# A filter bank turned earlier, PSUM banks in three pools, and a last stage that moves its final sums from SBUF to SBUF

## The chip, the core and the metric

The kernel runs on one core of a Trainium2 chip. The metric is device time in microseconds of one launch. One execution was also recorded by the hardware profiler; its "span" runs from the first to the last instruction. In what follows PE is TensorE, DVE is VectorE, ACT is ScalarE, POOL is GpSimd, and SP is the engine that issues nearly all DMAs; each takes its instructions in order. Tensors named `ud`, `xa`, `md`, `me` and `yd` lie in DRAM; all else that is named is in SBUF or, with a prefix `ps` or `p`, in PSUM. All numbers are float32.

## The reference, cut to what matters

The input is 8 sequences of 1024 tokens with 128 channels. Three blocks follow each other, each with a residual: a cosine-similarity attention of 4 heads, two state-space scans (forward and backward), and a spectral filter layer. The change touches the last one, and the last one only:

```python
Vf = jnp.fft.rfft(phi, n=n, axis=0)                 # 16 filters
Uf_p = jnp.fft.rfft(u, n=n, axis=1)                 # tokens, normalised
U_plus = jnp.fft.irfft(Vf[None, :, :, None] * Uf_p[:, :, None, :], n=n, axis=1)[:, :sl]
...
out = jnp.einsum('btkd,k,kde->bte', U_plus, s, Mpp) # and the same with (-1)^t
out = out + sum_i einsum('btd,de->bte', shift(u, i), Mu[i])   # 3 taps
x = t + out
```

So each of 16 filters convolves every channel causally over the whole sequence, a 128 x 128 matrix per filter mixes the channels, and the filters' results are added up.

## The kernel before, in words

The kernel exchanges the order: it mixes the filters first. For each of 128 frequencies it builds a 128 x 128 matrix (real and imaginary part, for both halves of the sequence), multiplies the spectra of the tokens by it, and transforms the product back. A sequence is cut into 2 blocks (`NB`, index `k`) of 512 tokens, and these into 4 interleaved parts (`r` or `q`) of 128. The tail of `fast_kernel` does this in two parts, and inside both the programs of all five engines are in the order in which the code is written (`manual_schedule(engines=ALL_IN_ORDER)`), so a place in the code is a place in each engine's queue.

**Spectra (pools `f_...`, from L1611).** A loop runs over the sequences b = 2 to 8. `transform(b)` (L1641) turns the normalised tokens on PE (`cpt`), and for each block multiplies them by the Fourier table `fwd` (`pf`); ACT and DVE take the results out, POOL adds them to the spectrum `sp`, and `store_spectra` writes it to `ud`. `copy_turned` (L567, two ACT copies) brings the turned tokens to `ut`, for the 3 taps (`taps_of`, L602, `pu`), whose sums DVE adds to the residual `X` (L612), and `store_residual` (L615) writes that to `xa`. In PSUM, `ps_f` has two buffers of two banks, `ps_o` two of one bank, `ps_t` one of two banks.

Between these, the 16 filters' matrices are prepared in four banks: `turned(n)` (L1624) transposes bank n on PE (`mdt`), DVE copies it (`me`), SP stores it to `me` in DRAM, and `spread(n)` (L1634) loads it back into its place in `mst` with four DMAs (L1636). `turned` runs at b = 3 to 6 between the two halves of the taps; `spread` at b = 4 to 7, first thing in the pass. So on SP the order of a pass is: `mst` of one bank, `ud`, `me` of the next bank, `xa`. In the pass b = 8 the first two of the eight steps of chunk 0's frequency matrices are made (L1595, PE; `gs` copies by ACT L1608 and DVE L1606), and these need all of `mst`.

**The loop over chunks (pools `g_...`, from L1708).** The 128 frequencies are in 16 chunks of 8. In a pass the matrices of the next chunk are made (`matrices`), 4 PSUM banks at a time, and between them come four products of this chunk (`apply`, L1727, `py`; n = 0 to 3, two to each half of the chunk's 8 frequencies). `gather` turns `py` into `sums`; `store` writes those of a half to `yd` (L1755), `fetch` (L1765) brings a part of them back with frequencies in partitions: only for piece 0, to `early_yt`. `amid_products` puts stores, fetches and the loads of the next spectra `u` (L1578) at a place on SP, by a wait for the middle of a product. A chunk holds every 16th frequency: its rows of `yd` and of `early_yt` lie 16 apart. All 8 PSUM banks are one pool, `g_ps_g`, which is opened when the three pools of the part before close.

**The last stage.** Four pieces (k, h), each of one block of four sequences: z = sums and differences of the piece's parts (DVE, L1831), 16 products by the inverse table `inv` (L1841, `pz`), DVE adds them to the residual (L1848), ACT issues the output's DMA (L1851). Pieces 1 to 3 are loaded from `yd` with two 1 MB DMAs each (L1825) into a room named `gs`; the residuals come from `xa` (L1782): 3 MB at the start of the last chunk, 1 MB behind piece 2.

Of the kernel before, what the change touches and what calls it, by code (L numbers as in the profile page):

```python
# [45 lines left out]
def fast_kernel(ctx: ExitStack, tc: tile.TileContext, a: dict, out: bass.AP, bad: bass.AP):  # L46
# [273 lines left out]
    def transforms(pool, tables):  # L320


        def over_2048(t):
            nc.vector.tensor_scalar(t, t, 1.0 / 2048.0, None, ALU.mult)

        odd = counted(pool, [2, NF // FC, FC], [[512, 2], [2, NF // FC], [2 * NF // FC, FC]], 1, 0, "odd")
        odd = odd.rearrange("p i c f -> p i (c f)")
        place = counted(pool, [4], [[1, 4]], 0, 4, "place")
        over_2048(place)
        by_place = [(fwd[:, k : k + 1], odd[:, 0:1, :], place[:, k : k + 1]) for k in range(4)]  # L330
        turns(by_place[:2])
        yield
        odd_row = counted(pool, [1], [[1, 1]], 1, 2, "odd_row")
        places = counted(pool, [4, P], [[1, 4], [4, P]], 0, 0, "places")
        over_2048(odd_row)
        yield
        turns(by_place[2:])
        yield
        for _ in angles(pool, fwd, "fwd"):
            yield  # L340
        yield
        turns([(inv, places, odd_row[:, 0:1])])
        for _ in angles(pool, inv, "inv"):
            yield
        yield
        lag = counted(pool, [2, 2], [[-256, 2], [1, 2]], 510, -2, "lag")
        over_2048(lag)
        for h in range(2):
            for r in range(2):
                t = pool.tile([P, 2, 2, NF], F32, name=f"lags{h}_{r}")  # L350
                turns([(t, odd, lag[:, h, r : r + 1])])
                for _ in angles(pool, t, f"lags{h}_{r}"):
                    pass
                tables.append(t)
                yield
        for t in tables:
            sines(t)

    def transform_taps(pool, ps, tables):
# [31 lines left out]
        nc.vector.tensor_reduce(sgn, late, AX.X, ALU.add)  # L391
        nc.vector.tensor_scalar(sgn, sgn, 1.0, None, ALU.add)
        nc.vector.tensor_tensor(weight[:, 1:2], weight[:, 0:1], sgn, ALU.mult)
        alt = pool.tile([P, NF // FC // 2, 2, FC], F32, name="alt")
        nc.gpsimd.memset(alt, 1.0)
        nc.gpsimd.memset(alt[:, :, 1], -1.0)
        alt = alt.rearrange("p c i f -> p (c i f)")

        both = pool.tile([P, NB, 512], F32, tag="work_w", name="taps_s")
        for m in range(NB):  # L400
# [191 lines left out]
    def store_spectra(b, sp):  # L592
        nc.sync.dma_start(
            ud[:, :, b].rearrange("c p k i q f -> p c (k i q f)"), sp.rearrange("p c k i q f -> p c (k i q f)")
        )
# [16 lines left out]
        nc.vector.scalar_tensor_tensor(xq[:, k], po, keep[:, k : k + 1], xq[:, k], ALU.mult, ALU.add)  # L612

    def store_residual(b):
        nc.sync.dma_start(xa[b].rearrange("p k r c -> p (k r) c"), X[b])  # L615

# [934 lines left out]
    with ExitStack() as s:  # L1553
# [10 lines left out]
            return u  # L1564

        def behind(instruction, other):
            tc.add_manual_dep(
                instruction.ins,
                other.ins.name,
                mybir.DependencyInfo(mybir.DependencyClass.Sync, mybir.DependencyReason.DATA),  # L1570
                reason="a place in the quarter",
            )

        def load_part(u, c, part, other=None):

            k, h = divmod(part, 2)
            bs = slice(4 * h, 4 * h + 4)
            t = nc.sync.dma_start(  # L1578
                u[:, 0, k, bs].rearrange("p b i f -> p b (i f)"), ud[c][:, bs, k].rearrange("p b i q f -> p b (i q f)")
            )  # L1580
            if other:
                behind(t, other)
            nc.gpsimd.tensor_scalar(u[:, 1, k, bs, 0, :], u[:, 0, k, bs, 1, :], -1.0, None, ALU.mult)  # L1583
            nc.gpsimd.tensor_copy(u[:, 1, k, bs, 1, :], u[:, 0, k, bs, 0, :])

# [25 lines left out]
        with ExitStack() as s2:  # L1611
# [8 lines left out]
                mds[n] = pm.tile([P, 8, C], F32, tag="md", name=f"md{n}")  # L1620
                nc.sync.dma_start(mds[n], md.rearrange("d r k e -> d (r k) e")[:, n::4, :])

            def turned(n):

                if n == 0:
                    load_bank(3)
                pt = ps_t.tile([P, 8, C], F32, tag="t", name=f"mdt{n}")
                for i in range(8):
                    nc.tensor.transpose(pt[:, i, :], mds[n][:, i, :], ident)
                to = p2.tile([P, 8, C], F32, tag="me", name=f"me{n}")  # L1630
                nc.vector.tensor_copy(to.rearrange("p k d -> p (k d)"), pt.rearrange("p k d -> p (k d)"))
                nc.sync.dma_start(me[:, n], to)

            def spread(n):  # L1634
                for g in range(4):
# [5 lines left out]
            def transform(b):  # L1641
# [7 lines left out]
                for k in range(NB):  # L1649
                    pf = ps_f.tile([P, 4, 2, NF], F32, tag="f", name=f"pf{b}_{k}")  # L1650
                    sd = p2.tile([P, 2, 2, 2, NF], F32, tag="sd", name=f"sd{b}_{k}")
                    later = p2.tile([P, 2, 2, NF], F32, tag="later", name=f"later{b}_{k}")
                    for _ in block_spectra(k, un, pf, sd, later, sp):
                        pass
                store_spectra(b, sp)
                copy_turned(uts[b], pt)

            def taps_of(b, k):
                po = ps_o.tile([P, 4, C], F32, tag="o", name=f"pu{b}_{k}")
# [23 lines left out]
            for b in range(2, B + 1):  # L1683
# [10 lines left out]
                if b > 2:  # L1694
                    taps_of(b - 1, 0)
                ahead(b, 1)
                if 3 <= b <= 6:
                    turned(b - 3)
                if b > 2:
                    taps_of(b - 1, 1)  # L1700
# [8 lines left out]
        with ExitStack() as s2:  # L1709
# [1 line left out]
            p3 = s2.enter_context(tc.tile_pool(name="g_3", bufs=3))  # L1711
            second_gs = s2.enter_context(tc.tile_pool(name="g_g", bufs=1))
            yp = s2.enter_context(tc.tile_pool(name="g_y", bufs=1, side="right"))
            early_yt = yp.tile([P, 2, 4, 4, C], F32, name="early_yt")
            ps_g = s2.enter_context(tc.tile_pool(name="g_ps_g", bufs=8, space=PSUM))

            def single_banks(c, n):
                return [ps_g.tile([P, 4, P], F32, tag="g", name=f"pg{c}_{n}_{g}") for g in range(4)]

            def apply(c, n, q, gs, u, py):  # L1720

# [27 lines left out]
                nc.vector.tensor_tensor(sums[:, 1, :], both[:, 0, :], both[:, 1, :], ALU.subtract)  # L1749
                stored[c, n] = sums  # L1750

            def store(c, n, other=None):

                at = c + n * 4 * chunks
                t = nc.sync.dma_start(  # L1755
                    yd[at :: chunks][:4].rearrange("f k b i q e -> f (k b i) (q e)"),
                    stored.pop((c, n)).rearrange("p q e -> p (q e)"),
                )
                if other:
                    behind(t, other)  # L1760

            def fetch(c, i, other=None):

                rows = slice(c, NF, chunks)
                t = nc.sync.dma_start(early_yt[rows, i], yd[rows, 0, 0:4, i])  # L1765
                if other:
                    behind(t, other)

            def amid_products(c, n, made):

                if n == 0 and c > 0:
                    store(c - 1, 1, made)
                if n == (3 if c + 1 < chunks else 2):
                    store(c, 0, made)
                if c + 1 < chunks and n in (1, 2):
                    for part in (2 * n - 2, 2 * n - 1):
                        load_part(us[c + 1], c + 1, part, made)
                if c > 0 and n > 1:
                    fetch(c - 1, n - 2, made)

            def load_residuals(k, b, n):
                nc.sync.dma_start(  # L1782
                    res[k][:, b : b + n].rearrange("p b r c -> p b (r c)"),
                    xa[b : b + n, :, k].rearrange("b p r c -> p b (r c)"),
                )

            chunks = NF // FC
            gathered, stored = {}, {}
# [1 line left out]
            for c in range(-1, chunks):  # L1790
# [4 lines left out]
                else:  # L1795
# [1 line left out]
                    room = chunk_matrices(c + 1, first_gs)  # L1797
                    res = [room[:, :32, :], mp.tile([P, 32, C], F32, tag="mst", name="res1")]
                    res = [t.rearrange("p (b r) c -> p b r c", b=B) for t in res]
                    load_residuals(1, 0, B)  # L1800
                    load_residuals(0, 0, 4)

                for n in range(4):
                    if c + 1 < chunks:
# [2 lines left out]
                                matrices(c + 1, i, gs[c + 1], single_banks(c + 1, i))  # L1807
                    if c >= 0:
                        half, turn = divmod(n, 2)
                        py = ps_g.tile([P, 2, C], F32, tag="g", name=f"py{c}_{n}")  # L1810
                        amid_products(c, n, apply(c, half, turn, gs[c], us[c], py))
                        apply(c, half, turn + 2, gs[c], us[c], py)
                        gather(c, half, turn, py)
            store(chunks - 1, 1)
            for i in range(2):
                fetch(chunks - 1, i)


            pieces = [(k, h) for k in range(NB) for h in range(2)]
            yts = [early_yt]  # L1820
            for n, (k, h) in enumerate(pieces[1:], 1):

                yts.append(room[:, 32 * n : 32 * n + 32].rearrange("p (i b q) c -> p i b q c", i=2, b=4))
                for i in range(2):
                    nc.sync.dma_start(yts[n][:, i], yd[:, k, h * 4 : h * 4 + 4, i])  # L1825
                if n == 2:
                    load_residuals(0, 4, 4)
            for yt, (k, h) in zip(yts, pieces):
                z = (second_gs if h else first_gs).tile([P, 2, 2, 4, C], F32, tag="u", name=f"z{k}_{h}")
                for r, i, op in ((0, 0, ALU.subtract), (0, 1, ALU.add), (1, 0, ALU.add), (1, 1, ALU.subtract)):  # L1830
                    nc.vector.tensor_tensor(z[:, r, i], yt[:, i, :, 2, :], yt[:, 1 - i, :, 3, :], op)  # L1831
# [3 lines left out]
                for b in range(0, 4, size):  # L1835
                    bs = slice(b, b + size)
                    to = res[blk][:, h * 4 + b : h * 4 + b + size]
                    for r in (0, 2, 1, 3):
                        po = ps_g.tile([P, 4, C], F32, tag="g", name=f"pz{k}_{h}_{b}_{r}")[:, :size]
                        for i in range(2):  # L1840
                            nc.tensor.matmul(  # L1841
                                po,
# [820 lines left out]
```

## Time and profile before

| | us |
|---|---|
| median of 3 runs (range) | 1401.44 (1399.33 to 1406.55) |
| the profiled execution | 1398.1 |
| its span | 1396.4 |
| PE busy in the span | 1324.2 (95%) |
| PE busy, 1140 to 1300, in the loop over chunks | 159.77 of 160 |
| PE busy, 1060 to 1100, entry to the loop | 34.95 of 40 |
| PE busy, 1300 to 1340 / 1340 to 1360 | 38.21 of 40 / 2.36 of 20 |
| PE busy, 1360 to 1380 / 1380 to the end | 20.00 of 20 / 9.23 of 16.4 |

A line of the timeline gives the start and length in us, the engine, the line of the kernel, what is written and read (partitions x elements), how many instructions were merged, and in brackets the idle time ahead of it with what ended it. SPq and ACTq lines are issues of DMAs by SP and ACT: their length is that of the issuing, not of the transfer. `[... <-issue]` means that the engine waited for nothing that the profile shows. In the view of stretches, each row has the busy time (and count) of PE, PE's weight loads, DVE, ACT and POOL, and then PE's granted clock (1 is full speed), the mean busy share of the 16 DMA engines, and GB/s.

### The profile page before, as it was taken

How to read it: one execution, taken by the hardware profiler on the slowest of the kernel's cores; microseconds unless marked ns; L12 is line 12 of the kernel's file. 1: busy time of each engine (PE TensorE's matmuls, PEld its weight loads, DVE VectorE, ACT ScalarE, POOL GpSimd, SP SyncE). 2: the span in 40 equal slices, each digit the busy share in tenths (PEclk: the TensorE clock that was granted, in tenths of full speed). 3: DMA queues.
4: the chain of work that ended last, by engine and by line, in shares of the span. 5: the costliest groups of instructions: out<-in, count | busy, mean ns of one | idle time of the engine just before them, and what ended most of it. 6: DMA issues, size and time to landing. Idle time of an engine off the chain costs nothing. (4 is left out here: it accounts for less than half of the span.)

```text
span 1396.4 us, 47738 instructions
## 1 busy us (share of the span) xinstructions
PE 1324.2 (95%) x20926; PEld 839.8 (60%) x20926; DVE 1102.8 (79%) x2144; ACT 922.4 (66%) x1428; POOL 552.4 (40%) x606
## 2 busy tenths in 40 slices
PE   7999999999999899999999999998998999999947
PEld 3333333333333566666666666666897999999934
DVE  5789889788868688889898888899764777777725
ACT  4766666766757788888888888886452555555510
POOL 3411986876910343434343433442883111111100
PEclk8999999999999999999999999999999999999979
DMA  7100111111000533444444543442476232333258
GB/s 182 47 2 2 35 43 39 54 39 39 24 9 12 126 77 78 108 93 103 96 107 95 120 92 92 93 92 61 141 246 203 52 74 75 76 75 81 73 173 301
DMA packets 143168, 123.25 MB, mean 88 GB/s; under 512 B 45000, under 2 KB 122440, under 8 KB 138856
## 3 DMA queue, kind: packets, MB, share of 16 engines
q1 hardware_dynamic: 140824, 115.93, 32.2%
q8 instruction: 166, 2.72, 0.8%
q10 hardware_dynamic: 2128, 4.19, 0.8%
q14 instruction: 50, 0.41, 0.1%
HBM read 78.15 MB, written 34.08 MB: 80 GB/s over the span
## 5 line engine op out<-in xcount | busy, mean ns | idle before, releaser
L810 ACT ACTIVATE pr<-pt 128x1024 f32<-128x1024 f32 x256 | 248.2, 1021 | 106.5 <-PE pt L805 105.5
L1608 ACT COPY gs<-pg 128x512 f32<-128x512 f32 x256 | 132.5, 602 | 67.7 <-PE pg L1595 67.0
L835 DVE TENSOR_TENSOR two<-pr,pr 128x1024 f32<-128x1024 f32 x128 | 164.9, 1329 | 15.5 <-ACT pr L810 15.5
L1606 DVE COPY gs<-pg 128x512 f32<-128x512 f32 x256 | 158.8, 685 | 18.9 <-PE pg L1595 10.8
L805 PE MATMUL pt<-q,k 32*128 32x512 f32 x1024 | 163.7, 656 | 6.1 <-ACT pr L810 4.2
L1595 PE MATMUL pg<-taps,mst 32*128 32x128 f32 x4096 | 148.1, 280 | 5.5 <-DMA mst<-me 2.9
L1595 PEld LDWEIGHTS pg<-taps,mst 32*128 32x128 f32 x4096 | 134.5, 187 | 19.2 <-issue 12.1
L826 PE MATMUL po<-pr,v 128*32 128x512 f32 x1024 | 141.1, 612 | 0.0
L1727 PE MATMUL py<-gs,u 128*32 128x128 f32 (+1 forms) x4096 | 128.4, 277 | 2.7 <-issue 2.7
L1031 POOL TENSOR_TENSOR ec<-ec,ct 128x2048 f32<-128x2048 f32 x16 | 83.6, 5227 | 112.4 <-ACT ct L1111 49.8
L1073 DVE SCALAR_TENSOR_TENSOR xs<-xp,cw,xs 128x1024 f32<-128x1024 f32 x96 | 122.5, 1282 | 2.2 <-issue 0.2
L1583 POOL TENSOR_SCALAR u<-u 128x128 f32<-128x128 f32 x64 | 34.2, 534 | 223.7 <-DMA u<-ud 188.6
L1727 PEld LDWEIGHTS py<-gs,u 128*32 128x32 f32 (+1 forms) x4096 | 112.1, 140 | 10.5 <-issue 2.9
L1095 PE MATMUL pb<-bxt,wbc 128*128 128x512 f32 x256 | 114.0, 597 | 3.6 <-ACT zs L1086 3.6
L805 PEld LDWEIGHTS pt<-q,k 32*128 32x128 f32 x1024 | 50.2, 188 | 89.7 <-ACT pr L810 27.2
L1303 POOL TENSOR_TENSOR rms<-rms_v,mhalf 128x8 f32<-128x8 f32 x16 | 26.6, 1660 | 157.0 <-DVE rms_v L1301 157.0
L1194 DVE SCALAR_TENSOR_TENSOR state<-state,dec,pst 128x64 f32<-128x64 f32 x448 | 87.3, 275 | 1.1
L1095 PEld LDWEIGHTS pb<-bxt,wbc 128*128 128x128 f32 x256 | 47.1, 189 | 60.4 <-issue 55.0
L826 PEld LDWEIGHTS po<-pr,v 128*32 128x32 f32 x1024 | 27.8, 110 | 89.7 <-issue 86.4
L1017 POOL TENSOR_TENSOR lm<-cs,lm 128x2048 f32<-128x2048 f32 x16 | 57.9, 3621 | 57.8 <-DVE xs L1073 34.7
L846 PE MATMUL pd<-two,ones 128*32 128x512 f32 x512 | 74.1, 617 | 2.4 <-DVE two L835 2.2
L1027 ACT ACTIVATE lm<-lm 128x1024 f32<-128x1024 f32 x64 | 65.7, 1052 | 6.6 <-POOL lm L1017 6.4
(310 smaller groups left out, 2786.9 us busy)
## 6 DMA issues: line engine op xcount, KB each, us to landing
lm<-cd SPq DMA_DIRECT2D x32, 512.0 KB
ec<-cd SPq DMA_DIRECT2D x32, 512.0 KB
ud<-sp SPq DMA_DIRECT2D x8, 1024.0 KB
u<-ud SPq DMA_DIRECT2D x64, 128.0 KB
yd<-sums SPq DMA_DIRECT2D x32, 256.0 KB
moved<-state SPq DMA_DIRECT2D x48, 128.0 KB
gs<-yd SPq DMA_DIRECT2D x6, 1024.0 KB
X<-in_x SPq DMA_DIRECT2D x8, 512.0 KB
```

The source lines that it names most:

```text
L805: nc.tensor.matmul(pt[:, i, :], lhsT=k[rows, j * P : (j + 1) * P], rhs=q[rows, cols], start=True, stop=True)
L810: nc.scalar.activation(pr[:, 2 * g : 2 * g + 2, :].rearrange("p i t -> p (i t)"), pt.rearrange("p i t -> p (i t)"), AF.Exp, scale=SCALE,)
L826: nc.tensor.matmul(po[rows, :], lhsT=vs[b][:, j, rows], rhs=pr[:, h, :], start=(j == 0), stop=(j == NT - 1))
L835: nc.vector.tensor_tensor(two, sums["pr"][:, 2 * g : 2 * g + 2, :], pr[:, 2 * g : 2 * g + 2, :], ALU.add)
L1031: t = nc.gpsimd.tensor_tensor(u.ec, u.ec, u.ct.unsqueeze(1).to_broadcast([P, NH, NT, L]), ALU.mult)
L1073: u.convolved = nc.vector.scalar_tensor_tensor(acc, xp[:, at : at + T], cw[u.d][:, n, i : i + 1], acc, ALU.mult, ALU.add)
L1095: nc.tensor.matmul(u.pb[:, i * 512 : (i + 1) * 512], lhsT=wbc[u.d][:, k, :], rhs=xt[:, at : at + 512], start=(k == 0), stop=(k == KC - 1),)
L1194: nc.vector.scalar_tensor_tensor(u.state[:, k, h, :], u.state[:, k - 1, h, :], u.dec[:, c, h, j : j + 1], u.pst[c][:, j, h, :], ALU.mult, ...
L1595: nc.tensor.matmul(pts[g][:, e, :], lhsT=mst[rows, n * 4 + e, :], rhs=taps[rows, cols].rearrange("p f q m i -> p (f q m i)"), start=True, ...
L1606: nc.vector.tensor_copy(to, frm)
L1608: nc.scalar.copy(to, frm)
L1727: product = nc.tensor.matmul(py[t * 32 : t * 32 + 32 - 16 * m, q // 2, :], lhsT=u[:, i, m:, :, :, q * FC + f].rearrange("p k b i -> p (k b ...
```

## The change

1. In the pass b = 2, `copy_turned` stands between the two blocks' spectra instead of behind both.
2. Bank 3 is turned in the pass b = 6 between the two blocks' spectra (`turned(3, True)`), instead of between the taps: into two `ps_o` banks instead of `ps_t`, with one half copied by ACT and the other by DVE. On SP its store comes ahead of the spectra's store of that pass.
3. The loop's eight banks come from three pools of 4, 2 and 2 banks and are used by turns; the first ones used are those of the last pool.
4. The frequencies are in natural order, so that a chunk is 8 neighbouring rows of `yd` and `early_yt` (`odd` and `alt` follow this). A half chunk's store is one run of 128 rows, a chunk's fetch is one DMA of 8 rows of 16 KB.
5. In the last chunk the 2 MB residual load is cut in two, put at products 0 and 2; the first half's sums are fetched at product 3. The last half's sums go from `sums` to `early_yt` by four DMAs from SBUF to SBUF (`move`), and to `yd` behind them. Piece 1 is loaded by two DMAs: rows 0 to 123 from SP at once, the last four rows from ACT behind the store. Pieces 2 and 3 are one DMA each, with 1 MB of residual behind each.

Both programs have the same products on PE and the same sums on DVE. Three changes of the diff (`store_residual`, the store of `me`, and where `behind` tests for a missing instruction) give the same instructions as before.

```diff
-        odd = counted(pool, [2, NF // FC, FC], [[512, 2], [2, NF // FC], [2 * NF // FC, FC]], 1, 0, "odd")
-        odd = odd.rearrange("p i c f -> p i (c f)")
+        odd = counted(pool, [2, NF], [[512, 2], [2, NF]], 1, 0, "odd")
...
-            def turned(n):
+            def turned(n, amid=False):
...
+                if amid:
+                    pts = [ps_o.tile([P, 4, C], F32, tag="o", name=f"mdt{n}_{i}") for i in range(2)]
+                else:
+                    pt = ps_t.tile([P, 8, C], F32, tag="t", name=f"mdt{n}")
+                    pts = [pt[:, 4 * i : 4 * i + 4] for i in range(2)]
                 for i in range(8):
-                    nc.tensor.transpose(pt[:, i, :], mds[n][:, i, :], ident)
+                    nc.tensor.transpose(pts[i // 4][:, i % 4, :], mds[n][:, i, :], ident)
                 to = p2.tile([P, 8, C], F32, tag="me", name=f"me{n}")
+                if amid:
+                    nc.scalar.copy(to[:, :4], pts[0])
+                    nc.vector.tensor_copy(to[:, 4:], pts[1])
...
                     for _ in block_spectra(k, un, pf, sd, later, sp):
                         pass
+                    if k == 0 and b == 2:
+                        copy_turned(uts[b], pt)
+                    if k == 0 and b == 6:
+                        turned(3, True)
                 store_spectra(b, sp)
-                copy_turned(uts[b], pt)
+                if b > 2:
+                    copy_turned(uts[b], pt)
...
-                if 3 <= b <= 6:
+                if 3 <= b <= 5:
                     turned(b - 3)
...
-            ps_g = s2.enter_context(tc.tile_pool(name="g_ps_g", bufs=8, space=PSUM))
+            banks = []
+            for n in (4, 2, 2):
+                ps_g = s2.enter_context(tc.tile_pool(name=f"g_ps_{len(banks)}", bufs=1, space=PSUM))
+                banks = [ps_g.tile([P, 4, C], F32, tag=f"pg{i}", name=f"pg{len(banks)}_{i}") for i in range(n)] + banks
...
-                at = c + n * 4 * chunks
-                t = nc.sync.dma_start(
-                    yd[at :: chunks][:4].rearrange("f k b i q e -> f (k b i) (q e)"),
+                at = c * FC + n * 4
+                t = engine.dma_start(
+                    yd[at : at + 4].rearrange("f k b i q e -> (f k b i) (q e)"),
...
+            def move(c, n, yt, piece):
+                at = c * FC + n * 4
+                for f in range(4):
+                    rows = stored[c, n][f * 32 + piece * 8 : f * 32 + piece * 8 + 8]
+                    nc.sync.dma_start(
+                        yt[at + f : at + f + 1].rearrange("p b i q e -> p (b i) (q e)"),
+                        rows.rearrange("x q e -> x (q e)"),
+                    )
...
             def amid_products(c, n, made):
+                last = c + 1 == chunks
                 if n == 0 and c > 0:
                     store(c - 1, 1, made)
-                if n == (3 if c + 1 < chunks else 2):
+                if n == 3 and c > 0:
+                    fetch(c - 1, 0, FC, made)
+                if n == (2 if last else 3):
                     store(c, 0, made)
+                if last and n == 3:
+                    fetch(c, 0, 4, made)
+                if last and n in (0, 2):
+                    load_residuals(1, 2 * n, 4, made)
...
-            store(chunks - 1, 1)
-            for i in range(2):
-                fetch(chunks - 1, i)
...
+            move(chunks - 1, 1, yts[0], 0)
+            store(chunks - 1, 1, None, nc.sync)
+            def load_piece(n, rows, engine):
+                k, h = pieces[n]
+                engine.dma_start(
+                    yts[n][rows].rearrange("p b i q c -> p (b i q c)"),
+                    yd[rows, k, h * 4 : h * 4 + 4].rearrange("f b i q e -> f (b i q e)"),
+                )
+            load_piece(1, slice(0, NF - 4), nc.sync)
+            load_piece(1, slice(NF - 4, NF), nc.scalar)
+            for n in range(2, 4):
+                load_piece(n, slice(0, NF), nc.sync)
+                load_residuals(0, 4 * n - 8, 4)
```

## The prediction

> **What bounds the kernel now.** I read the busy shares first (PE 95% of 1396.4 us), then busy time by stretches, which shows where PE is not busy: the two ends of the stage that the change touches. So I read the timeline there. First its beginning, PE alone:
>
> ```profile
> 1006.71 1.09 PE L562 MATMUL cpt<-ident,ln_x 128*128 128x128 f32 x8 [1.66 <-ACT ut L567]
> ...
> 1053.33 8.20 PE L602 MATMUL pu<-m_u,ut 128*128 128x128 f32 x72
> 1063.88 0.79 PE L1595 MATMUL pg<-taps,mst 32*128 32x128 f32 x2 [2.35 <-DMA mst<-me]
> 1065.23 3.79 PE L1595 MATMUL pg<-taps,mst 32*128 32x128 f32 x30 [0.56 <-DMA mst<-me]
> 1068.96 3.70 PE L602 MATMUL pu<-m_u,ut 128*128 128x128 f32 x24
> 1072.59 1.17 PE L1595 MATMUL pg<-taps,mst 32*128 32x128 f32 x32
> 1075.75 9.71 PE L1595 MATMUL pg<-taps,mst 32*128 32x128 f32 x256 [2.00 <-DVE gs L1606]
> ```
>
> Between 1007 and 1061.5 PE has no gap. At 1061.53 it waits for the last filter bank (`mst`): 32 products that take 1.17 us at 1072.59 take until 1068.96, so 6.3 us go. At 1073.8 it waits again, for PSUM banks. The queue on SP tells why the bank is late:
>
> ```profile
> 1050.48 2.80 SPq L1636 DMA_DIRECT2D mst<-me  x4
> 1053.39 0.41 SPq L593 DMA_DIRECT2D ud<-sp  x1
> 1053.89 3.39 SPq L1632 DMA_DIRECT2D me<-me  x1
> 1057.33 0.84 SPq L615 DMA_DIRECT2D xa<-X  x1
> 1060.96 2.80 SPq L1636 DMA_DIRECT2D mst<-me  x4
> ```
>
> The bank's store `me` was ready at 1047.7, stands behind the spectra's store and, following it, takes 3.39 us to issue; it has landed only at 1060.96.
>
> Then the end, all engines:
>
> ```profile
> 1340.95 0.65 PE L1727 MATMUL py<-gs,u 128*16 128x128 f32 x13 [2.66 <-issue]
> ...
> 1342.58 0.28 DVE L1749 TENSOR_TENSOR sums<-both 128x128 f32<-128x128 f32 x1
> 1348.29 1.31 SPq L1765 DMA_DIRECT2D early_yt<-yd  x2
> 1349.65 0.54 SPq L1755 DMA_DIRECT2D yd<-sums  x1
> 1355.61 1.20 SPq L1765 DMA_DIRECT2D early_yt<-yd  x2
> 1356.86 2.29 SPq L1825 DMA_DIRECT2D gs<-yd  x4
> ...
> 1358.29 6.56 PE L1841 MATMUL pz<-early_yt,inv 128*128 128x512 f32 x8 [16.69 <-DMA early_yt<-yd]
> ```
>
> The last sums exist at 1342.86; they leave at 1349.65, are in memory at 1355.6 and back at 1358.29: PE stands for 16.69 us. From 1358.29 to the span's end it is 38.1 us: piece 0 takes 9.83 (to 1368.12), pieces 1 to 3 take 6.87 each, 2.0 pass before piece 3 (its data, landed at 1383.9), and 5.7 for the last sum and output. Busy time by stretches:
>
> ```profile
> 1344.00:1348.00 4.00, 0.00 (x0) 0.00 (x0) 0.00 (x0) 0.00 (x0) 0.00 (x0) 0.50 0.26 101
> 1360.00:1364.00 4.00, 4.00 (x6) 1.69 (x5) 2.87 (x5) 0.00 (x0) 0.00 (x0) 0.50 1.04 396
> 1364.00:1368.00 4.00, 4.00 (x10) 1.71 (x9) 1.50 (x2) 0.00 (x0) 0.00 (x0) 0.99 1.05 384
> ```
>
> The last three columns are PE's clock, DMA share and GB/s. While only stores of sums run, 0.26 of 16 engines (4.2) move 101 GB/s, 24 each; with the pieces all 16 move about 390, 24.4 each.
>
> [...] here a fetch issued by 1356.2 lets PE go at 1358.29, 2.1. [...]
>
> **The change, part by part.** Times are on the old profile's scale (span 1396.4, execution 1398.1; the median of the runs shown is 1401.44, and I move it by the same difference).
>
> (a) Sequence 2's copies to `ut` go between its two spectra. They are two ACT copies, 1.08 us together, issued while PE does the second block; PE's 1.66 us wait at 1006.71 falls away. Gain 1.6 (bounds 0 and 1.66). PE is gapless behind it, so it carries.
>
> (b) Bank 3 is turned amid sequence 6. The eight transposes (1.04 us) stay on PE, in another place. One 1.22 us DVE copy becomes an ACT copy of about 0.59 (the row of L580, same size) and a DVE copy of about 0.65; ACT waits 3.2 us and DVE 2.58 in that place. Without that cover it would be 0.9. The two `ps_o` banks used are free: their reader ran at 1038.64. What counts is SP: `me` now stands before `ud`, right behind the `mst` that ends at 1053.28; the 3.39 us issue falls on `xa`, which nobody awaits yet. Then 1053.28 + 0.5 (`me`) + 0.41 + 3.39 = 1057.6 is where the last `mst` can start, 3.3 earlier than 1060.96. Its bytes stand behind 1.5 MB of `ud` and `xa` (to about 1060 at the 320 to 330 GB/s that the trace shows for them), so I take 2.5 (bounds 0 and 3.4). PE also sinks less into the slow clock: the 3.70 us at 1068.96 was 2.84 elsewhere, 0.9. Together 3.4.
>
> (c) Three pools instead of one: the first banks of the loop are `ps_t`'s and `ps_o`'s, which need not wait for the evictions of `ps_f`. PE's 2.00 us wait goes; behind it DVE's evictions set the pace (9.69 us unbroken from 1076.99, after 1.29 idle), so 1.3 (bounds 0 and 2). SP's `u` loads follow the last taps, which come earlier too.
>
> (a) to (c): 6.3.
>
> (d) The loop: PE has no waits there (0.5 us in 15 chunks). Frequencies of a chunk now lie together, so the store is 128 x 512 (16 engines) and two fetches become one. Hidden behind 16.4 us chunks: nothing. The tables made early are as large as before, and the same banks turn in the same order.
>
> (e) The end. The 2 MB residual load is split, half to the first and half to the third product of the last chunk; the 1 MB one goes behind the pieces. So the store of the chunk's first half no longer stands behind 3 MB, and its fetch issues in time. PE's 2.66 us "issue" gap at 1340.95 lies where all 16 engines were full; I give half back: 1.3. The last sums are then ready at 1341.55. Four moves follow on SP at 0.55 us (between store 0.54 and fetch 0.60), then the store, 0.54: 1344.3. The fourth move ends its issue at 1343.75, so piece 0 starts at about 1346.3, 12 us earlier.
>
> But piece 1 is next: 124 rows on SP, four on ACT behind the store. [...] It is 124 x 16 KiB = 2.03 MB at 100 GB/s, 20.3 us, where the old form took about 5. First bytes 1.45 us after issue (as from 1355.61 to 1357): 1345.75 + 20.3 = 1366.05. [...] landing 0.7: 1370.1. PE has been idle since 1356, so its clock is half again: 9.83 + 6.87 + 6.87 and 5.7 for the end, 29.3: 1399.4. [...] So the end loses 3.0.
>
> Sum: -6.3 + 3.0 = -3.3: 1398.
>
> **Rivals.** (1) Piece 1 runs on 16 engines: the end is bound by PE or all the bytes alike: 1346.3 + 36.1 = 1382.4, so -14.0 - 6.3 = -20: 1381. For it: the pieces run on all engines today; [...] (2) Slower: the four engines give less than 100 GB/s. The one place is piece 1's flow. From 1352 to 1355 the lone four-engine store moved 72. Below 86 GB/s (23.6 us) the kernel is slower than before, below 66 by 0.5%; at 65 it takes 31 us: 1409. Against: loads reach 24.4 per engine. (3) Four engines, with better luck: no "issue" gap (1.3), the first output not in the way (2.6): 1394 or less; a bound of (b) at 3.4 brings 1393. (4) `mst` comes no earlier because its bytes stand in line: (b) gives nothing, 1401.5.
>
> **How the numbers follow.** Under 0.5%, 7 us, a measurement of this kernel can hardly tell from no change. Chances: the forecast 0.48, its own range 1391 to 1405; (1) 0.14; (2) 0.10; (3) 0.22; (4) 0.06. Faster: (1) and (3), 0.36; same: forecast and (4), 0.54; slower: (2), 0.10. The range must take in (1) to hold eight in ten beside misses of the others: 1380 to 1406.
>
> **What would show it.** Right: PE starts `pz` from `early_yt` near 1340 (6 earlier than 1346), then waits some 14 us for `gs<-yd`, in which the DMA share falls to about 0.25 and 100 GB/s; `mst` waits on PE under 3 us; no 1.66 at `cpt`. Wrong: share 1.0 through piece 1, or a wait at another place, say for the fetch that SP issues ahead of the moves.

## The result, and the profile after

The changed kernel takes 1423.03 us (median of 6 runs, 1417.48 to 1429.35), the kernel before in the same comparison 1400.76 (6 runs, 1398.18 to 1406.55). The ratio is 1.0159, with a 95% interval of 1.0124 to 1.0194: 1.6% slower. I had forecast 1398 and a range of 1380 to 1406, so the forecast missed the sign and the range. The profiled execution took 1427.88, 4.9 above its median.

First the page of the changed kernel: the span, PE's busy time, and the lines of the chain that ended last.

```profile
span 1426.2 us, 47749 instructions
PE 1330.2 (93%) x20926; PEld 843.0 (59%) x20926; DVE 1103.6 (77%) x2144; ACT 922.8 (65%) x1429; POOL 550.5 (39%) x606
...
PE pg L1594 10%; PE pg L1749 9%; DMA gs<-yd 3%; PE pu L601 3%; PE pf L571 2%; PE pg L1886 2%; DVE state L1193 1%; PE spo L1272 0%; DVE xs L1072 0%; PE cpt L561 0%; DMA mst<-me 0%; DVE b_shift L477 0%; DVE gs L1605 0%; PE pz L1039 0%; PE sb L1140 0%
```

PE's busy time is nearly that of before (1324.2). In the chain stands a transfer, `gs<-yd`, with 3% of the span, some 43 us: the loads of the pieces of the last stage. (The chain of the kernel before reaches back only to 1383.88 and can't be set beside it.) The end of the timeline, lines of PE, SP and DVE, shows where it stands:

```profile
1345.30 0.64 PE L1749 MATMUL pg<-gs,u 128*16 128x128 f32 x12 [2.92 <-issue]
...
1346.93 0.28 DVE L1771 TENSOR_TENSOR sums<-both 128x128 f32<-128x128 f32 x1
1347.24 2.75 SPq L1797 DMA_DIRECT2D early_yt<-sums  x4
1350.04 0.45 SPq L1777 DMA_DIRECT2D yd<-sums  x1
1350.59 1.99 SPq L1862 DMA_DIRECT2D gs<-yd  x2
1351.95 6.04 PE L1886 MATMUL pg<-early_yt,inv 128*128 128x512 f32 x8 [6.00 <-DMA early_yt<-sums]
1353.88 10.73 SPq L1803 DMA_DIRECT2D gs<-xa  x1
...
1397.23 5.59 PE L1886 MATMUL pg<-gs,inv 128*128 128x512 f32 x8 [35.81 <-DMA gs<-yd]
...
1406.09 3.60 PE L1886 MATMUL pg<-gs,inv 128*128 128x512 f32 x8
...
1412.96 1.89 PE L1886 MATMUL pg<-gs,inv 128*128 128x256 f32 x8
```

Piece 0 starts 4.74 us after the last sums (ready at 1347.21), where it was 15.43 before. Then PE stands for 35.81 us for piece 1, whose load was issued at 1350.59: 46.6 us to its use. Pieces 2 and 3 (1406.09, 1412.96) are there by then. SP needs 10.73 us to issue its last residual load. Two stretches of the same execution, in the view with all engines; the last three columns are again PE's clock, the busy share of the 16 DMA engines and GB/s:

```profile
1354.00:1388.00 34.00, 7.42 (x14) 2.85 (x13) 3.48 (x5) 0.00 (x0) 0.00 (x0) 0.60 1.00 206
...
1400.00:1404.00 4.00, 4.00 (x10) 1.80 (x9) 1.50 (x2) 0.00 (x0) 0.00 (x0) 0.86 0.26 103
```

For 34 us all 16 engines are busy, and they move 206 GB/s; the kernel before moved 384 to 396 with the same share. Then a share of 0.26 is left, four engines' work, at 103 GB/s.

The entry to the loop, PE:

```profile
1007.07 1.09 PE L561 MATMUL cpt<-ident,ln_x 128*128 128x128 f32 x8
...
1053.91 8.20 PE L601 MATMUL pu<-m_u,ut 128*128 128x128 f32 x72
1065.13 0.71 PE L1594 MATMUL pg<-taps,mst 32*128 32x128 f32 x4 [3.02 <-DMA mst<-me]
1066.00 0.71 PE L1594 MATMUL pg<-taps,mst 32*128 32x128 f32 x4 [0.16 <-DMA mst<-me]
1067.21 2.89 PE L1594 MATMUL pg<-taps,mst 32*128 32x128 f32 x28 [0.51 <-DMA mst<-me]
1070.03 4.55 PE L601 MATMUL pu<-m_u,ut 128*128 128x128 f32 x24
...
1077.67 8.51 PE L1594 MATMUL pg<-taps,mst 32*128 32x128 f32 x224 [1.09 <-DVE gs L1605]
1086.12 2.02 PE L1749 MATMUL pg<-gs,u 128*32 128x128 f32 x64
```

and SP's issues in the same stretch:

```profile
1052.14 2.80 SPq L1643 DMA_DIRECT2D mst<-me  x4
1055.05 0.40 SPq L1639 DMA_DIRECT2D me<-me  x1
1055.55 0.38 SPq L592 DMA_DIRECT2D ud<-sp  x1
1055.98 4.72 SPq L614 DMA_DIRECT2D xa<-X  x1
1060.79 3.29 SPq L1643 DMA_DIRECT2D mst<-me  x4
```

The wait of 1.66 at `cpt` is gone, but PE still waits 3.7 us for the filter bank (2.9 before), and the 24 products at 1070.03 take 4.55 (3.70 before). The granted clock is 0.50 from 1070 to 1072 and 0.65 to 1074; before it was 0.50 from 1068 to 1070 and 0.86 to 1072.

To compare stretches I count from a point ahead of the change, the first `spo` of the last sequence (965.33 before, 967.47 after; in the other executions it lies between 958.6 and 964.7, so the 2.1 us are not put down to the change). To the first product of the loop it is 120.06 us before and 118.65 after: 1.4 gained. From there to the last products of the loop it is 255.56 and 259.18: 3.6 lost. From the last sums to the end it is 53.5 (1342.86 to 1396.4) and 79.0: 25.5 lost. With the 2.1 that makes the 29.8 by which the spans differ.

### The profile page after: what moved, and what is told of

It is laid out like the page before. It is cut to its first block, busy times and chain, and to the rows that moved or that the text cites. A ratio compares the mean times of both kernels' runs of the same rounds, so it can differ in the third digit from the quotient of the medians.

```text
span 1426.2 us, 47749 instructions
## 1 busy us (share of the span) xinstructions
PE 1330.2 (93%) x20926; PEld 843.0 (59%) x20926; DVE 1103.6 (77%) x2144; ACT 922.8 (65%) x1429; POOL 550.5 (39%) x606
## 5 line engine op out<-in xcount | busy, mean ns | idle before, releaser
L834 DVE TENSOR_TENSOR two<-pr,pr 128x1024 f32<-128x1024 f32 x128 | 165.2, 1331 | 15.6 <-ACT pr L809 15.6
L1749 PE MATMUL pg<-gs,u 128*32 128x128 f32 (+1 forms) x4096 | 128.7, 277 | 3.2 <-issue 3.2
L1749 PEld LDWEIGHTS pg<-gs,u 128*32 128x32 f32 (+1 forms) x4096 | 112.2, 141 | 10.7 <-issue 3.2
```

Of the source, the lines that this page charges most:

```text
L834: nc.vector.tensor_tensor(two, sums["pr"][:, 2 * g : 2 * g + 2, :], pr[:, 2 * g : 2 * g + 2, :], ALU.add)
L1749: product = nc.tensor.matmul(py[t * 32 : t * 32 + 32 - 16 * m, q // 2, :], lhsT=u[:, i, m:, :, :, q * FC + f].rearrange("p k b i -> p (k b ...
```

## The experiments

Kernels of one group ran on the same chip with the same runs of the kernel before, whose median was 1398.31 us (e1 to e4), 1398.58 (e5 to e8), 1400.15 (e9, e10) and 1396.27 (e11, e12). Across groups the ratios are to be compared.

| kernel | median, us | ratio to before (95% interval) |
|---|---|---|
| changed kernel | 1423.03 | 1.0159 (1.0124 to 1.0194) |
| e1: cut at 112 | 1386.80 | 0.9925 (0.9900 to 0.9949) |
| e2: cut at 124, 2 KB runs | 1412.73 | 1.0103 (1.0073 to 1.0133) |
| e3: 128 rows whole | 1383.53 | 0.9902 (0.9868 to 0.9935) |
| e4: start of the change only | 1395.49 | 0.9986 (0.9974 to 0.9997) |
| e5: cut at 124, loaded alone | 1409.30 | 1.0101 (1.0055 to 1.0146) |
| e6: cut at 120 | 1390.49 | 0.9942 (0.9927 to 0.9956) |
| e7: cut at 64 | 1394.33 | 0.9981 (0.9962 to 0.9999) |
| e8: e3 with an earlier bank | 1381.62 | 0.9885 (0.9851 to 0.9919) |
| e9: e3 without the moves | 1387.15 | 0.9900 (0.9871 to 0.9930) |
| e10: cut at 112, all on SP | 1387.15 | 0.9919 (0.9890 to 0.9948) |
| e11: cut at 112, behind the store | 1387.26 | 0.9936 (0.9910 to 0.9963) |
| e12: cut by columns | 1384.48 | 0.9901 (0.9865 to 0.9936) |

### Is it the 124 rows, or the long runs?

Two things are new in piece 1's load: 124 rows, which I had estimated to go to four engines (e5 below shows a share of 0.25 to 0.27), and runs of 16 KB instead of 2 KB. Cut at 112 (e1):

```diff
-            load_piece(1, slice(0, NF - 4), nc.sync)
-            load_piece(1, slice(NF - 4, NF), nc.scalar)
+            load_piece(1, slice(0, NF - 16), nc.sync)
+            load_piece(1, slice(NF - 16, NF), nc.scalar)
```

> Piece 1 is cut at row 112 instead of 124, nothing else: 112 rows from SP and 16 from ACT[...]. Theory F (the 124 rows go over four engines, and these four hold up everything): piece 1 lands some 8 us after its issue, before PE has ended piece 0, so PE's wait of 35.8 us goes, and from piece 0 to the end it takes the 36.1 us that I worked out instead of 74.2: 38 us less than the changed kernel, about 1385. Theory L (it is the 16 KB runs: the trace of the changed kernel shows all engines busy at about 200 GB/s where 2 KB runs gave 390): the rate stays near 200 GB/s, the 8.2 MB of pieces, residuals and first output take 41 us, PE waits for pieces 2 and 3 instead: about 1400.

1386.80 us: 0.9925 of before. PE's lines of e1:

```profile
1344.38 5.68 PE L1886 MATMUL pg<-early_yt,inv 128*128 128x512 f32 x8 [6.76 <-DMA early_yt<-sums]
...
1354.77 3.67 PE L1886 MATMUL pg<-gs,inv 128*128 128x512 f32 x8 [1.27 <-DMA gs<-yd]
```

A shift of twelve rows from one DMA to the other turns the wait of 35.81 into 1.27. That is theory F. The other side of the pair keeps the cut at 124 and takes the runs back to 2 KB (e2):

```diff
-                engine.dma_start(
-                    yts[n][rows].rearrange("p b i q c -> p (b i q c)"),
-                    yd[rows, k, h * 4 : h * 4 + 4].rearrange("f b i q e -> f (b i q e)"),
-                )
+                for i in range(2):
+                    engine.dma_start(yts[n][rows, :, i], yd[rows, k, h * 4 : h * 4 + 4, i])
```

with the order of `i` and `b` in the tile exchanged to match.

> The cut at row 124 stays, and pieces 1 to 3 go back to runs of 2 KB (two DMAs for each piece, as in the kernel before). Theory F: no change against the changed kernel, PE waits some 36 us for piece 1, about 1420. Theory L: the rate of the shared stretch goes back to 390 GB/s, piece 1 is bound by its own 20.3 us on four engines as I had forecast, PE waits some 14 us: about 1402.

1412.73 us, between the two. SP and PE of e2:

```profile
1344.70 25.01 SPq L1863 DMA_DIRECT2D gs<-yd  x4
...
1362.88 2.04 PE L1884 MATMUL pg<-gs,inv 128*128 128x512 f32 x2 [7.37 <-issue]
1382.23 5.46 PE L1884 MATMUL pg<-gs,inv 128*128 128x512 f32 x6 [17.30 <-DMA gs<-yd]
```

Piece 1 comes in two DMAs here. PE uses the first half at 1362.88, after 7.37 us idle, and the second only after another 17.30: 37.5 us from issue to use (1344.70 to 1382.23). That it is less than 46.6 goes with something that I had not expected: SP needs 25.01 us for its four issues, those of pieces 1 and 2, and issues piece 3 only from 1374.85, so pieces 2 and 3 come late and share less of the time (share 0.26, at 66 to 75 GB/s, from 1348 to 1356). So e2 does not part the two theories cleanly; Theory L falls with e3, which has 16 KB runs and reaches 428 GB/s.

### Where the limit lies: 128 rows in one

e3 gives up the early start. Piece 1 is one DMA on SP, behind the store of the last sums:

```diff
-            load_piece(1, slice(0, NF - 4), nc.sync)
-            load_piece(1, slice(NF - 4, NF), nc.scalar)
+            load_piece(1, slice(0, NF), nc.sync)
```

> Piece 1 is one DMA of 128 rows, on SP behind the store of the last sums, nothing on ACT. Theory F: 16 engines; the load waits about 2 us for the store, lands about 1360 on the trace's scale, PE still finds it when piece 0 ends at 1361.8: about 1385, the same as the cut at 112. Theory L: 200 GB/s with 16 KB runs, about 1400.

1383.53 us, 0.9902: 1.0% faster than before. PE goes from piece 0 to piece 1 without a wait. Two stretches of e3, 4 us each, counted from the issue of the load (here without the other engines' columns):

```profile
1343.51:1347.51 4.00, 3.89 (x5) 0.50 0.81 287
1347.51:1351.51 4.00, 4.00 (x10) 0.95 1.01 428
```

This is my rival (1), with the four engines taken away: it stood at 1381, a gain of 20 us where e3 has 14.8.

### How much is the four engines' own, how much is sharing?

In e5 the cut at 124 stays, and all that follows on SP waits until the 124 rows have landed:

```diff
-            load_piece(1, slice(0, NF - 4), nc.sync)
+            first = load_piece(1, slice(0, NF - 4), nc.sync)
...
-                load_piece(n, slice(0, NF), nc.sync)
+                behind(load_piece(n, slice(0, NF), nc.sync), first)
```

> The changed kernel with its cut at 124, but the loads of pieces 2 and 3 and the residual loads behind them are issued only when piece 1's 124 rows have landed; piece 1 so has its four engines nearly to itself. Theory S (the 44 us come from sharing: while pieces 2, 3 and the residuals flow, all engines run at half rate): piece 1 moves at about 100 GB/s as the four engines did after 1390 in the changed kernel, 20.3 us and the 1.5 around it, landing 22 to 24 us after its issue against 46; PE waits some 12 us; the later pieces follow at once on 16 engines; about 1398. Theory O (31 rows on each of four engines are slow of themselves, as the 66 to 75 GB/s of the short runs' version between 1348 and 1356 hints): landing 30 to 45 us after its issue: 1406 to 1422.

1409.30 us. SP's line, where the second of the two DMAs waits for the first, and stretches of e5:

```profile
1343.14 34.56 SPq L1862 DMA_DIRECT2D gs<-yd  x2
```

```profile
1348.00:1352.00 4.00, 4.00 (x8) 0.66 0.27 74
1352.00:1356.00 4.00, 3.13 (x8) 1.00 0.25 82
...
1372.00:1376.00 4.00, 0.00 (x0) 0.50 0.12 38
...
1384.00:1388.00 4.00, 4.00 (x10) 1.00 1.10 441
```

Even with nothing of the other pieces in flight, the 124 rows take some 34 us. The share of 0.25 to 0.27 is four engines; they give 74 to 82 GB/s, not 100, and they do not end together: at 1372 two of them are left (0.12). Theory O. What sets the rate stays open: in e2 shares of 0.26 moved 66 to 75 GB/s from 1348 to 1356, and one of 0.27 moved 102 from 1360 to 1364. The output of piece 0 runs beside it (from 1356), as I had counted in the forecast. So of the 46.6 us in the changed kernel, 25.8 are what I forecast, some 8 are the four engines' lower rate and unequal end, and some 12 are sharing with pieces 2, 3 and the residuals. Once these 128-row loads are alone, they run at 404 to 441 GB/s (1380 to 1388).

### Why do all engines slow down?

In the changed kernel the loads of 128 rows ran at half rate too while piece 1 was under way, and in e1 the first 8 us gave 285 GB/s against e3's 357 (means of two stretches of 4 us from the issue; all that was in flight counts). Not every transfer beside piece 1 was slow. In e5 the first output, 128 rows stored from SBUF, was issued at 1355.95, while the 124 rows were still under way:

```profile
1356.00:1360.00 4.00, 0.00 (x0) 0.69 0.78 286
```

That is 22.9 GB/s for each busy engine, where the changed kernel's 206 from 1354 to 1388 are 12.9. Only loads were seen to slow down; no run varies this alone. Two more cuts. In e6:

```diff
-            load_piece(1, slice(0, NF - 4), nc.sync)
-            load_piece(1, slice(NF - 4, NF), nc.scalar)
+            load_piece(1, slice(0, 120), nc.sync)
+            load_piece(1, slice(120, NF), nc.scalar)
```

> Piece 1 cut at 120: [...] If the number of engines decides: as with the cut at 112 (1387) or with 128 rows (1384), no wait over 1.5 us for piece 1. The cut at 112 moved only 242 to 266 GB/s between 1344 and 1352, where 128 rows moved 328 to 444. Theory R (7 rows for each engine are no even share, 8 are): here 330 or more, and 1384. Theory Q (rows on two queues at once slow each other): again about 250, and 1387.

In e7 the same with 64:

> Piece 1 cut in halves: 64 rows from SP, 64 from ACT behind the store[...]. Theory R: an even share, 330 GB/s or more in the first 8 us, about 1384. Theory Q: two queues at once, and more of it on the second one: about 250 or less, 1387 or more.

e6 is at 0.9942, e7 at 0.9981; PE waits 5.06 and 6.34 us for piece 1. From e6, then from e7, counted from the issue of the load:

```profile
1352.51:1356.51 4.00, 4.00 (x8) 0.74 1.17 201
```

```profile
1348.49:1352.49 4.00, 4.00 (x8) 0.73 0.90 238
```

Neither 120 nor 64 rows help: at shares of 1.17 and 0.90 both rates are below the 266 of the cut at 112 in the same stretch (share 1.06), and from its issue to its use piece 1 takes 15.6 us in e6 and 17.8 in e7, against 12.3 in e1; e7 is slower in time as well. (e6 issued the load 3.9 us behind the store; part of its 5.06 may be that.) Theory R falls. Q is still possible, so e10 has the 16 rows of e1 on SP too:

```diff
-            load_piece(1, slice(NF - 16, NF), nc.scalar)
+            load_piece(1, slice(NF - 16, NF), nc.sync)
```

> Piece 1 cut at 112, with the last 16 rows on SP behind the 112 and the store instead of on ACT: all loads in one queue. Theory Q (loads on the queues of SP and ACT at once run at 250 GB/s where one queue gives 330 to 440): over 330 GB/s in the stretch of piece 1, no wait for it, about 1384. If the slow stretch comes from the cut itself, or from loading while the store of the sums runs: 250 GB/s again, a wait of 1 to 5 us, 1387 to 1392.

e11 is e3 with its one load cut, so that both parts stand behind the store:

```diff
-            load_piece(1, slice(0, NF), nc.sync)
+            load_piece(1, slice(112, NF), nc.sync)
+            load_piece(1, slice(0, 112), nc.sync)
```

> Piece 1 in two loads on SP as in the run before, 16 rows and 112 rows, but both behind the store of the last sums, as the whole 128 rows stood. Theory C (a cut into row counts other than 128 is what halves the rate, on one queue or two): 200 to 280 GB/s over the first 8 us of the loads again. Theory T (it is loading while the sums' store is still running): 330 to 440 GB/s, as with the 128 rows. Time near 1385 in both; the rate decides.

e12 is e3 with piece 1 cut by columns, two loads of 128 rows with 8 KB each:

```diff
-                engine.dma_start(
-                    yts[n][rows].rearrange("p b i q c -> p (b i q c)"),
-                    yd[rows, k, h * 4 : h * 4 + 4].rearrange("f b i q e -> f (b i q e)"),
-                )
+                for d in range(0, 4, 2 if n == 1 else 4):
+                    size = 2 if n == 1 else 4
+                    engine.dma_start(
+                        yts[n][rows, d : d + size].rearrange("p b i q c -> p (b i q c)"),
+                        yd[rows, k, h * 4 + d : h * 4 + d + size].rearrange("f b i q e -> f (b i q e)"),
+                    )
```

> Piece 1 in two loads on SP behind the store as well, but cut by columns: 128 rows of 8 KB each. Theory C: 330 to 440 GB/s[...]. If two loads for one piece are what costs: 200 to 280. Time near 1384.

The second stretch of 4 us from the issue, in e10, e11 and e12:

```profile
1344.78:1348.78 4.00, 4.00 (x7) 0.57 1.12 287
```

```profile
1344.29:1348.29 4.00, 4.00 (x10) 0.94 1.06 307
```

```profile
1348.85:1352.85 4.00, 4.00 (x8) 0.72 1.06 446
```

The means of the first 8 us are 296 GB/s in e10, 230 in e11, 359 in e12 and 357 in e3. Over the first 12 us it is 262 in e1, 172 in e6, 259 in e7, 278 in e10 and 263 in e11, all cut by rows, against 371 in e12, 366 in e3 and, with 128 rows whole too, 352 in e9 (below). One queue is as slow as two (Q falls), loading behind the store is as slow as beside it (T falls), two loads cut by columns are as fast as one. What makes the difference is the cut by rows (C). In time these kernels do not differ beyond their intervals, since piece 0 hides most of it; the rate decides, in one profiled execution each.

No profile here tells the engines or their paths apart. Why a cut by rows lowers the rate, and why the loads of 128 rows go at half rate beside piece 1, stays open; that the cut by rows goes with the lower rate is shown, in the executions above.

### The start of the stage

e4 is the kernel before with parts (a), (b) and (c) alone: `turned` as in the change, the loop's banks from `bank()` in place of the single pool, and

```diff
+                    if k == 0 and b == 2:
+                        copy_turned(uts[b], pt)
+                    if k == 0 and b == 6:
+                        turned(3, True)
                 store_spectra(b, sp)
-                copy_turned(uts[b], pt)
+                if b > 2:
+                    copy_turned(uts[b], pt)
...
-                if 3 <= b <= 6:
+                if 3 <= b <= 5:
                     turned(b - 3)
```

> The kernel before with parts (a), (b) and (c) of the change alone: the copies of sequence 2, bank 3 amid sequence 6 and the three pools; order of frequencies, loop and end are the old ones. My forecast for these three parts was 6.3 us: about 1394.5. The trace of the changed kernel, in which PE still waits 3.7 us for the last bank and 1.1 for the evictions, says about 1.3: 1399.5.

0.9986 (0.9974 to 0.9997): 2.0 us, at most 3.6. PE's lines:

```profile
1002.54 1.09 PE L562 MATMUL cpt<-ident,ln_x 128*128 128x128 f32 x8
...
1060.81 0.71 PE L1595 MATMUL pg<-taps,mst 32*128 32x128 f32 x4 [3.23 <-DMA mst<-me]
...
1073.19 8.51 PE L1595 MATMUL pg<-taps,mst 32*128 32x128 f32 x224 [1.09 <-DVE gs L1606]
```

Again no wait at `cpt`, 3.4 us for the bank (a second wait of 0.16 follows), 1.09 for the evictions. From `spo` to the loop it takes 118.77 us; 119.15, 118.64, 118.98 in e1, e2, e3, against 120.06 before. In all twelve executions with this start, the changed kernel's among them, it is 118.6 to 120.4, half of them below 118.9: a gain of some 1.2, and in e6 none.

e8 asks whether it is the bytes ahead of the bank. It is e3 with the bank's loads right behind its store:

```diff
                     if k == 0 and b == 6:
                         turned(3, True)
+                        spread(3)
...
-                if 4 <= b <= 7:
+                if 4 <= b <= 6:
                     spread(b - 4)
```

> The version with piece 1 as one DMA of 128 rows (1384), and the loads of the last filter bank moved on SP: right behind its store amid sequence 6, ahead of that sequence's spectra store and the residual store, instead of behind both. Theory M (what was wrong with part (b): the bank's bytes stand in line behind 1.5 MB of those two stores, so that an earlier issue alone gives almost nothing): PE's 3.8 us wait for the bank goes, and about 1.2 of the slow clock behind it, so 4 to 5 us less: about 1379. If instead the chain store, landing, load is what takes the time: no difference, 1384.

1381.62 us, 0.9885. SP's lines of e8:

```profile
1049.98 0.40 SPq L1639 DMA_DIRECT2D me<-me  x1
1054.74 2.78 SPq L1643 DMA_DIRECT2D mst<-me  x4
1057.62 0.41 SPq L592 DMA_DIRECT2D ud<-sp  x1
```

With nothing of its own sequence ahead, the bank's store still needs 4.4 us to land (1050.38 to 1054.74), and PE still waits 2.1 us (3.8 in e3). From `spo` to the loop it is 117.49 us, 1.5 less than e3 and less than in any of the twelve. Theory M gets a third of what it promised: from the store's issue to PE's first product with the bank it is still 8.2 us, and PE was ready 6.7 us after that issue. The time itself does not tell e8 from e3.

### What the moves are worth

PE's wait for piece 0 fell by 10.7 us in the changed kernel. Two edits above all could do that: the moves, and the residual loads that no longer stand ahead of the sums. e9 is e3 with the moves taken out:

```diff
-            move(chunks - 1, 1, yts[0], 0)
             store(chunks - 1, 1, None, nc.sync)
+            fetch(chunks - 1, 1, 4, None)
```

> The version with piece 1 as one DMA of 128 rows (1384), without the four moves: the last half's sums are stored and their four rows of piece 0 fetched from memory, as in the kernel before, but with the residual loads where the change puts them. Theory V (the moves from SBUF to SBUF are what brings PE's wait for piece 0 from 16.7 to some 7 us): the wait is long again, 12 to 16 us: 1389 to 1393. Theory W (it is the 3 MB of residuals that stood ahead of the sums and no longer do): store 0.5 + about 2.2 to landing, fetch 0.3 + 2.1: 5.1 after the sums against the moves' 4.75 in the changed kernel: within 1 us of 1384.

PE and SP of e9:

```profile
1342.20 0.34 SPq L1777 DMA_DIRECT2D yd<-sums  x1
1348.26 0.25 SPq L1786 DMA_DIRECT2D early_yt<-yd  x1
...
1352.40 6.02 PE L1885 MATMUL pg<-early_yt,inv 128*128 128x512 f32 x8 [11.93 <-DMA early_yt<-yd]
```

Piece 0 starts 10.67 us after the sums (1341.73), against 5.83 in e3 and 15.43 before. So in this pair the moves bring 4.8 (in the executions with moves it is 4.7 to 8.0, so 2.6 to 5.9), and what e9 keeps about as much: the residuals' place, with the new form of stores and fetches, which no run takes apart. Neither theory alone is right. Theory W failed at the store: 256 KB took 5.7 us to land, not 2.2; as it was issued other transfers were in flight (332 GB/s from 1340 to 1344). The medians, 0.9900 and 0.9902, do not tell the two kernels apart.

## Why the prediction was wrong, step by step

**(e), piece 1: the step that failed.** "It is 124 x 16 KiB = 2.03 MB at 100 GB/s, 20.3 us", and with it the landing at 1370.1, 25.8 us after the issue. That 124 rows go to four engines was an estimate, and right (shares of 0.25 to 0.27 in e5; the wait gone in e1, e3). The size was not: 46.6 us. The 100 GB/s came from 24 GB/s for each engine in two other shapes, a store and whole pieces, and I took them to hold for the 124 rows (e5: 74 to 82 GB/s, and a share that falls from 0.23 to 0.12 between 1364 and 1376), and to hold while 6 MB of other loads ran beside it (206 GB/s over all 16 engines). The 25.8 has 3.3 us, an estimate, for other transfers on the same four engines, which no profile here shows; it has nothing for the piece taking longer beside the other loads (46.6 against 34). From the sums to piece 1 it took 50.0 us (1347.21 to 1397.23), I had 28.55 (1341.55 to 1370.1): this one term is 21.5 of the 33.1 us by which the profiled span missed my sum (1426.2 against 1393.1). From piece 1 to the end I had 29.3, at half the clock at first; it took 29.0 (granted clock 0.50 from 1364 to 1400, 0.86 to 1404).

**Rival (2)** named the place: four engines under 100 GB/s, "at 65 it takes 31 us: 1409". e5, with the sharing taken away, comes out there, 34 us and 1409, in part by luck: its engines went at 74 to 82, and their unequal end made up the rest. I gave it 0.10 because loads had reached 24.4 per engine, all of them loads of 128 rows. It did not have the sharing, which makes the rest of the loss. **Rival (1)**, 16 engines, would have been some 5 us too good for e3.

**(e), piece 0: right, but the exact figure is luck.** 4.75 us after the sums; 4.74. Four moves took 0.69 each, not 0.55, which cost 0.6, and from the end of the fourth move's issue to PE it took 1.96 (1349.99, 1351.95), where the sum had 2.55. In the ten other executions with the moves it is 5.0 to 8.0. **(e), the "issue" gap: wrong.** I gave back 1.3 of 2.66; it was 2.92. In the other executions it was 1.83 (e1), 1.68 (e3), 1.92 (e4, old residual loads) and nothing in e5: it varies from one execution to the next, and no tie to the residual loads shows.

**(a): right**; the wait of 1.66 is gone in every kernel with this part. **(b): wrong**, and rival (4) nearly right: counted from `spo`, the bank's loads were issued 2.3 us earlier where I had 3.3, because `xa`, one place ahead of them, took 4.72 us to issue where I had moved 3.39 to it, and the loads themselves took 3.29 for 2.80; PE had the bank 0.9 earlier. Meanwhile PE came to the bank 1.6 us sooner, mostly by (a), to wait for it. I had seen the 1.5 MB ahead and written it down as a bound of 0, and then took 2.5 plus 0.9 of clock. **(c): about right in size**: 1.09 is left of the 2.00 wait, 0.9 gained where I had 1.3. Together 1.4 where the sum had 6.3: 4.9 us of the miss. e4, with these parts alone, is 2.0 us faster than before, and the interval leaves no room for 6.3.

**(d): the loop.** The new store of 128 rows keeps 16 engines busy, as I had it: in the changed kernel one moves 369 to 410 GB/s at shares of 0.98 to 1.08 (1104.6 to 1105.0). For the loop I had forecast nothing; it took 3.6 us longer in the changed kernel, with scattered small delays. But e1 and e3, with the same loop, took 255.16 and 254.63 against 255.56 before. To the last sums it is 261.1 in the changed kernel, 257.5 before, and 255.6 to 259.6 in the eleven other executions with the new loop: so nothing shows it to be the change's. With the 1.3 of the gap it makes 4.9 of the miss, and the 2.1 ahead of the change the rest: 21.5 - 0.3 (the end) + 4.9 + 4.9 + 2.1 = 33.1.

**What would show it.** I had named a share of 0.25 and 100 GB/s through piece 1's wait. They came only after 1388; until then the share was 1.0, which I had put down as a sign of 16 engines. A full share was no sign of a full rate.

## What to carry to other kernels

Before cutting a DMA by rows to start part of it early, look at the row counts: a cut at 124 instead of 112 cost some 33 us here (1.0159 against 0.9925), and one whole load of 128 rows behind a short wait was as good as any cut, and faster in flow than all cuts by rows (352 to 366 GB/s over 12 us against 172 to 278). A rate for each engine was good for the shape it was taken from (24 GB/s in the store of before, 17 to 21 with the 124 rows of e5); read GB/s next to the busy share, since 16 busy engines moved 206 or 441 GB/s. And where several waits lie in line, as `cpt` and the bank, a gain at the first lengthened the second here (1.66 us gone at `cpt`, the bank's wait 3.7 where it was 2.9), and that one fell only with its own chain of store, landing and load (2.1 in e8).

## What the runs showed of the hardware that I had not expected

- Loads of 128 rows went at half rate while one of 124 rows ran beside them, with all engines busy: 206 GB/s in all over 34 us in the changed kernel, 404 to 441 in e5 once that one had landed. A store of 128 rows beside such a load did not: 286 GB/s in all at a share of 0.78 from 1356 to 1360 in e5, 22.9 for each busy engine, against 12.9.
- With a 2 MB load cut by rows (16 and 112), 262 to 278 GB/s were in flight over the first 12 us; with it cut by columns 371, whole 352 to 366.
- The four engines of a load of 124 rows ended at different times: the share fell from 0.23 (1364 to 1368) to 0.12 (1372 to 1376) in e5, so two of them were still at work 29 us after the issue.
- SP needed 25.01 us to issue two loads of 124 rows and two of 128 in runs of 2 KB, half a piece each (e2); the issues of pieces 1 and 2 took 0.81 together in e3, in whole loads with runs of 16 KB.
- A store of 128 x 512 numbers took 5.7 us to land in e9, with 332 GB/s in flight as it was issued, and 2.4 in e3, with 85 (means from 1340 to 1344).
